# Layer 0 of a two-layer graph network: maxima over two blocks instead of four, sums three blocks late, destination breaks made in pieces

## The chip, the cores and the metric

The kernel runs on one core of a Trainium2 chip. The core has five engines with their own instruction streams: PE (TensorE: matrix products and transposes), DVE (VectorE), ACT (ScalarE), POOL (GpSimd, which here issues the indirect gathers) and SP (SyncE, which here issues the plain transfers). Each engine takes its instructions in the order of the program and stops at the first that has to wait. The metric is the device time of one execution in microseconds.

## The reference

6250 nodes of 128 features, and 106250 edges sorted by destination (50000 drawn pairs in both directions, and a loop at each node). Two layers, each with a layer norm, a relu and a residual sum around it. Cut to what matters:

```python
# layer 0, attention over the edges of each destination
xl = x @ Wl + bl;  xr = x @ Wr + br;  e = edge_attr @ We
m = leaky_relu(xl[src] + xr[dst] + e, 0.2)
logits = m @ att
mx = segment_max(logits, dst)
ex = exp(logits - mx[dst])
den = segment_sum(ex, dst)
out = segment_sum(xl[src] * (ex / (den[dst] + 1e-16))[:, None], dst) + bias_out
h = gelu(x + out); batch norm over the nodes
# layer 1, messages
em = relu(layer_norm(concat(x[src], x[dst]) @ msg_w + msg_b)) * edge_weight
messages = segment_sum(em, dst) / (count + 1e-8)
h_new = relu(layer_norm(concat(x, messages) @ upd_w + upd_b));  gated mix with x
```

## The kernel before

The edges are padded to 128 x 832 and cut into 104 blocks of 1024 edges (8 tiles of 128; `NS` = 104, `ST` = 8). As the edges are sorted, the destinations of a block lie in a window of 126 nodes. The changed part is the loop over the rounds of layer 0. Round `s` works on block `s` for the logits and on block `u = s - LAG` for the sums:

- SP loads the window of `xr` (`W`), the destinations spread over all partitions (`dlb`) and a row of weights for block `s+2` (`load`, L851 to L859). DVE makes the transposed one-hot `oht` of it (`one_hot_t`, L863).
- POOL gathers eight tiles of `xl[src]` into `gl` (L196), from a pool of 10 buffers.
- PE multiplies `oht` with `W` into PSUM, eight products a block (`expand`, L867, called by `spread` for block `s+1`).
- DVE adds the gathered rows (L1033), ACT takes the Relu (L1034), DVE multiplies with att (L1051) and sums over the features (L1053): the logits. Each of these blocks of instructions stands where it is written in the loop, since the scheduling is manual.
- `maxima` turns the logits of `SB` = 4 blocks into exponents and run maxima: it transposes them (L900, PE), scans forward and backward over the runs of equal destinations (L907, L908, DVE), joins the runs across rows (L911 to L926), scans once more with what comes from the rows beside it (L929 to L933), takes Exp (L934, ACT), transposes back (L937, L938) and writes `exm` (L942 DVE, L944 ACT). It is a generator of eight pieces; a round takes two of them, one after the Relu and one at its end.
- The sums of block `u`: DVE makes the one-hot `oh` (L1040) and copies the pair of columns (L1043), ACT scales the gathered rows by the exponents, eight instructions (L1049), and PE multiplies (L1063). One round later `flush` copies the sum from PSUM (L1008, ACT) and SP stores it into one of two result tables.
- `nodes` joins the two tables for a group of four tiles of nodes once their blocks are stored, one step a round over seven rounds; `turn` transposes tiles of `x`.

`LAG` is SB + 3 = 7. `kbrk` holds the breaks between runs of equal destinations, one row per tile of a group of blocks, for the scans. Before the loop it is filled in four pieces of up to seven groups (L832, L833), then scaled (L835). The result tables are zeroed by 20 transfers per layer from SP (L848), in layer 0 four a round over the first five rounds. After the loop come a middle part (batch norm and the tables of layer 1) and layer 1, whose rounds have the same plan without maxima. They are not changed.

Of the kernel before, what the change touches and what calls it, by code (L numbers as in the profile page):

```python
# [30 lines left out]
ST = 8  # L31
SE = ST * P
NS = K // ST
SB = 4
NBT = SB * ST
BT = K // NBT
WIN = 126
# [11 lines left out]
def kernel(  # L49
# [36 lines left out]
    def flat(v, ap, offset=0):  # L86
        return bass.AP(tensor=v.tensor, offset=v.offset + offset, ap=ap)
# [86 lines left out]
    def over_tiles(row, n):  # L174
        return row[:, None, :].to_broadcast([P, n, D])
# [565 lines left out]
    def fast():  # L741
# [39 lines left out]
        att8 = fs.tile([P, D], F32, name="att8")  # L781
        V.tensor_scalar(att8, att_r, 0.8, None, op0=ALU.mult)
        g0 = ExitStack()
        gp = g0.enter_context(tc.tile_pool(name="e0g", bufs=10))
        with tc.tile_pool(name="col1", bufs=1) as p1, tc.tile_pool(name="rows", bufs=2) as rp, tc.tile_pool(
            name="ps_p", bufs=2, space=PSUM
        ) as ps_p:
            base_f = p1.tile([NS, 1], F32, name="base_f")
            V.tensor_copy(base_f, dst_r[:, 0:1])
            fr = rp.tile([NS, SE], F32, name="fr", tag="rows")  # L790
            V.tensor_scalar(fr, dst_r, base_f, None, op0=ALU.subtract)
            dl_b = p1.tile([NS, SE], BF16, name="dl_b")
            V.tensor_copy(dl_b, fr)
            nc.sync.dma_start(dl_d, dl_b)

            for w in Ws:
                nc.scalar.dma_start(w[WIN : WIN + 1], We)
                nc.scalar.dma_start(w[WIN + 1 : P], flat(br, [[0, 1], [1, D]]))
            for o in ohts:
                V.memset(o, 1.0)  # L800
            ends_i = p1.tile([1, 2, K], I32, name="ends_i")
            nc.scalar.dma_start(ends_i[:, 0, :], flat(dst, [[1, 1], [P, K]]))
            nc.scalar.dma_start(ends_i[:, 1, :], flat(dst, [[1, 1], [P, K]], P - 1))
            ea_r = rp.tile([NS, SE], F32, name="ea_r", tag="rows")
# [12 lines left out]
            fst = rp.tile([NS, SE], F32, name="fst", tag="rows")  # L817
            V.memset(fst[:, 0:1], 1.0)
            V.tensor_tensor(fst[:, 1:SE], dst_r[:, 1:SE], dst_r[:, 0 : SE - 1], ALU.not_equal)
            columns(ps_p, fst_c, fst, "ctp")  # L820
            ew_r = rp.tile([NS, SE], F32, name="ew_r", tag="rows")
            nc.sync.dma_start(ew_r, flat(edge_weight, [[SE, NS], [1, SE]]))
            columns(ps_p, ew_c, ew_r, "ctp")


            V.memset(kbrk[:, :, 0:1], 0.0)
            V.memset(kbrk[:, :, P : P + 1], 0.0)
            HB = 7
            for b in range(0, BT, HB):
                n = min(HB, BT - b)  # L830
                dst_n = p1.tile([NBT, HB, P], I32, name="dst_n")
                nc.sync.dma_start(dst_n[:, :n, :], flat(dst, [[P, NBT], [P * NBT, n], [1, P]], b * P * NBT))  # L832
                V.tensor_tensor(kbrk[:, b : b + n, 1:P], dst_n[:, :n, 1:P], dst_n[:, :n, 0 : P - 1],  # L833
                                ALU.not_equal)
            V.tensor_scalar(kbrk[:, :, 1:P], kbrk[:, :, 1:P], -BIG, None, op0=ALU.mult)  # L835
            V.memset(jn, 1.0)
            V.memset(kS, 1.0)
            V.memset(kR, 1.0)
            V.tensor_tensor(jn[:, 1:K], ends_i[:, 0, 1:K], ends_i[:, 1, 0 : K - 1], ALU.not_equal)
            V.tensor_tensor(kS[:, 1:K], ends_i[:, 1, 1:K], ends_i[:, 1, 0 : K - 1], ALU.not_equal)  # L840
            V.tensor_tensor(kR[:, 0 : K - 1], ends_i[:, 0, 1:K], ends_i[:, 0, 0 : K - 1], ALU.not_equal)
            for t in (jn, kS, kR):
                V.tensor_scalar(t, t, -BIG, None, op0=ALU.mult)

        def zero(tables, n, i):

            for r in tables:
                nc.sync.dma_start(r.rearrange("(p k) f -> p (k f)", p=P)[:, i * 5 * n : (i + 1) * 5 * n],  # L848
                                  zt[:, : 5 * n])
# [36 lines left out]
        with tc.tile_pool(name="e0", bufs=2) as ep, tc.tile_pool(  # L886
# [3 lines left out]
        ) as ps_m, tc.tile_pool(name="ps_1", bufs=1, space=PSUM) as ps_1, tc.manual_schedule():  # L890
            iota_ps = ps_1.tile([P, P], F32, name="iota_ps")
            S.copy(iota_ps, iota_f)
            LAG = SB + 3
            gls, lgc, exm, wins, pss, aggs = {}, {}, {}, {}, {}, {}

            def maxima(b):
# [46 lines left out]
                                fst_c[:, bs, :], ALU.mult)  # L943
                S.copy(em[:, :, :, 1], tz[:, 1, :].rearrange("p (s j) -> p s j", j=ST))  # L944
                exm[b] = em
                yield
                yield

            def nodes(g):
# [58 lines left out]
                S.copy(agg, aggs.pop(s))  # L1008
                store(agg, res0_d, s)

            steps, group = None, None
            due = rounds_of(LAG)
            turns = {r + 6: g for r, g in due.items() if g < NGR - 2}
            turns.update({3: NGR - 2, 8: NGR - 1, 13: NGR})
# [5 lines left out]
            for s in range(NS + LAG + 1):  # L1020
                u = s - LAG
                if s + 2 < NS:
                    wins[s + 2] = load(op_, xr_d, s + 2, True)
                if s < NS:
                    gl = gp.tile([P, ST, WL], F32, name="gl")
                    gls[s] = gl
                    for j in range(ST):
                        gather(gl[:, j, :], xl_d, src_c[:, s, j : j + 1])
                if s + 1 < NS:
                    spread(s + 1)  # L1030
                if s < NS:
                    ps = pss.pop(s)
                    V.tensor_tensor(ps, ps, gl[:, :, :D], ALU.add)  # L1033
                    S.activation(ps, ps, AF.Relu)  # L1034
                if steps is not None:
                    next(steps, None)
                if 0 <= u < NS:
                    b, q = divmod(u, SB)
                    oh = ep.tile([P, ST, P], F32, name="oh")
                    V.tensor_tensor(oh, over_tiles(iota_ps, ST), over_features(dl_c[:, u, :], ST),  # L1040
                                    ALU.is_equal)
                    glw = ep.tile([P, ST, W0], F32, name="glw")
                    V.tensor_copy(glw[:, :, D:], exm[b][:, q])  # L1043
                if u >= 1:
                    flush(u - 1)
                if 0 <= u < NS:
                    glu = gls.pop(u)
                    for j in range(ST):
                        S.activation(glw[:, j, :D], glu[:, j, :D], AF.Copy, scale=exm[b][:, q, j, 1:2])  # L1049
                if s < NS:  # L1050
                    V.tensor_tensor(ps, ps, over_tiles(att8, ST), ALU.mult)  # L1051
                    lr = small.tile([P, ST], F32, name="lr")
                    V.tensor_reduce(lr, ps, AX.X, ALU.add)  # L1053
                    V.tensor_add(lr, lr, gl[:, :, D])
                    if s % SB == 0:
                        lgc[s // SB] = mp.tile([P, SB, ST], F32, name="lgc")
                    V.tensor_add(lgc[s // SB][:, s % SB, :], lr, eac_c[:, s, :])
                if s + 2 < NS:
                    one_hot_t(*wins[s + 2])
                if 0 <= u < NS:  # L1060
                    aggs[u] = ps_1.tile([P, W0], F32, name="agg_ps")
                    for j in range(ST):
                        T.matmul(aggs[u], oh[:, j, :], glw[:, j, :], start=(j == 0), stop=(j == ST - 1))  # L1063
                if s < NS and s % SB == SB - 1:
                    steps = maxima(s // SB)
                    next(steps, None)
                elif steps is not None:
                    next(steps, None)
                if s < 5:
                    zero(res0_d, W0, 2 * s)  # L1070
                    zero(res0_d, W0, 2 * s + 1)
                if 20 <= s < 30:
                    zero(res1_d, WL, s - 20)
                if s == 30:
                    nc.sync.dma_start(b_d[NP:], zt[:, :D])
                if s in due:
                    group = nodes(due[s])
                if group is not None:
                    next(group, None)
                if s in turns:  # L1080
                    turn(turns[s])
# [303 lines left out]
```

## Time and profile before

| what | value |
|---|---|
| median of 11 runs | 2414.46 us (2405.15 to 2417.61) |
| profiled execution | 2408.61 us, span 2406.8 us |
| busy, share of the span | PE 57%, DVE 68%, ACT 53%, POOL 70% |
| mean granted TensorE clock | 0.766 |
| first gather of layer 0 | 71.3 us |
| first add of layer 0 | 99.7 us |
| last gather of layer 0 issued | 1139.4 us |
| last sums of layer 0 copied from PSUM | 1183.2 us |
| chain that ended last, by engine | POOL 44%, issue 18%, DVE 15%, DMA 13%, PE 6%, ACT 3% |

In the lines of the profile, L12 is line 12 of the kernel; `out<-in` are the names of the tiles; `xN` counts instructions; a bracket gives the idle time of the engine just before an instruction and what ended it. A line of the waits reads: who waited, for whom, microseconds in total, times, the longest. PE's granted clock is 1.00 at full and 0.50 at half speed.

### The profile page before, as it was taken

To read this page: it belongs to the slowest core of one execution; us is meant where nothing else is said; L and a number is where in the kernel's file an instruction comes from. 1 tells how busy PE (TensorE), PEld (TensorE's weight loads), DVE (VectorE), ACT (ScalarE), POOL (GpSimd) and SP (SyncE) were. 2 spreads that over 40 slices of the span, in tenths; PEclk is the share of its full clock that TensorE was granted. 3 is DMA by queue.
4 is the path that set the end of the run, shared out by engine and by line. 5 is a ranking of instruction groups with operands and counts; after the bars stand their busy time and mean duration, and the time that the engine had idled before them with its cause. 6 is when DMAs were issued, how large, how long until landed. Compare 5 with 4: busy or idle time off the path is not lost.

```text
span 2406.8 us, 30614 instructions
## 1 busy us (share of the span) xinstructions
PE 1372.7 (57%) x7692; PEld 1268.6 (53%) x7692; DVE 1635.9 (68%) x3597; ACT 1277.4 (53%) x4267; POOL 1695.0 (70%) x1703
## 2 busy tenths in 40 slices
PE   6445556556566556665584555555655655555553
PEld 3345555555555555555464555554554655555553
DVE  6666677677677767767545567767767767768765
ACT  5223343333344344334456667677677677667663
POOL 1677777777777777777057777777777777777770
PEclk9668877787878777777686777778778778877876
DMA  6844455444444444443142333343343343334331
GB/s 166 209 117 93 112 150 140 97 99 92 102 101 92 101 95 93 100 99 80 30 140 76 88 96 98 86 106 96 84 108 97 83 109 100 87 102 102 85 97 30
DMA packets 217495, 242.88 MB, mean 101 GB/s; under 512 B 41373, under 2 KB 158077, under 8 KB 217309
## 3 DMA queue, kind: packets, MB, share of 16 engines
q0 software_dynamic: 53792, 110.57, 22.1%
q1 hardware_dynamic: 160657, 130.00, 18.9%
q8 instruction: 63, 1.03, 0.2%
q14 instruction: 123, 1.01, 0.1%
q10 hardware_dynamic: 2860, 0.27, 0.1%
HBM read 197.43 MB, written 43.25 MB: 100 GB/s over the span
## 4 chain that ended last, share of the span: by engine, by line
POOL 44%; issue 18%; DVE 15%; DMA 13%; PE 6%; ACT 3%; POOLq 0%; DVEq 0%; another core or an unknown queue 0%; ACTq 0%; SPq 0%
POOL gl L196 44%; DMA gl<-xl_d,src_c 6%; DMA gl<-a_d,src_c 5%; DVE y L1314 3%; DVE m_ps L1033 2%; DVE y L1298 2%; DVE oh L1309 2%; PE agg_ps L1063 1%; DVE y L1316 1%; PE agg_ps L1329 1%; PE mm L1156 1%; ACT sq L1303 1%; DVE oht L863 1%; DMA src_r<-in_src_dram 1%; PE ctr L1126 1%
## 5 line engine op out<-in xcount | busy, mean ns | idle before, releaser
L196 POOL DMA_INDIRECT gl<-xl_d,src_c x832 | 815.7, 980 | 307.7 <-issue 234.7
L196 POOL DMA_INDIRECT gl<-a_d,src_c x832 | 845.7, 1016 | 260.6 <-issue 236.2
L1329 PE MATMUL agg_ps<-glw,oh 128*128 128x129 f32 x1664 | 362.4, 402 | 493.4 <-ACT glw L1320 454.0
L1329 PEld LDWEIGHTS agg_ps<-glw,oh 128*128 128x128 f32 x1664 | 334.8, 296 | 513.5 <-ACT glw L1320 513.5
L1063 PE MATMUL agg_ps<-glw,oh 128*128 128x130 f32 x1664 | 346.3, 390 | 379.3 <-ACT glw L1049 192.4
L1063 PEld LDWEIGHTS agg_ps<-glw,oh 128*128 128x128 f32 x1664 | 322.4, 291 | 396.4 <-ACT glw L1049 396.4
L1034 ACT ACTIVATE m_ps<-m_ps 128x1024 f32<-128x1024 f32 x104 | 104.8, 1008 | 567.1 <-DVE m_ps L1033 420.4
L1303 ACT ACTIVATE sq<-y 128x128 f32<-128x128 f32 x832 | 257.1, 309 | 274.7 <-DVE y L1298 251.1
L1033 DVE TENSOR_TENSOR m_ps<-m_ps,gl 128x1024 f32<-128x1024 f32 x104 | 128.2, 1232 | 295.3 <-DMA gl<-xl_d,src_c 273.9
L867 PE MATMUL m_ps<-W,oht 128*128 128x128 f32 x1664 | 262.4, 323 | 37.8 <-DVE oht L863 26.4
L867 PEld LDWEIGHTS m_ps<-W,oht 128*128 128x128 f32 x1664 | 246.9, 235 | 46.0 <-DVE oht L863 22.3
L1298 DVE TENSOR_TENSOR y<-y_ps,gl 128x1024 f32<-128x1024 f32 x104 | 126.9, 1220 | 190.5 <-DMA gl<-a_d,src_c 157.6
L1320 ACT ACTIVATE glw<-y,ew_c 128x128 f32<-128x128 f32 x832 | 254.5, 389 | 3.4
L1049 ACT ACTIVATE glw<-gl,exm 128x128 f32<-128x128 f32 x832 | 254.3, 394 | 0.0
L867 PE MATMUL y_ps<-W,oht 128*128 128x128 f32 x1664 | 227.3, 295 | 13.2 <-DVE oht L863 8.9
L867 PEld LDWEIGHTS y_ps<-W,oht 128*128 128x128 f32 x1664 | 223.6, 216 | 13.7 <-issue 13.7
L1314 DVE SCALAR_TENSOR_TENSOR y<-y,rs,mg_r 128x128 f32<-128x128 f32 x832 | 227.5, 345 | 0.0
L863 DVE TENSOR_SCALAR oht<-dlb,iota_p 126x1024 f32<-126x1024 bf16 x208 | 160.2, 770 | 12.7 <-DMA dlb<-dl_d 12.4
L1303 ACT ACTIVATION_READ_ACCUMULATOR sq<-y 128x1 f32 x832 | 155.0, 186 | 0.0
L1051 DVE TENSOR_TENSOR m_ps<-m_ps,att 128x1024 f32<-128x1024 f32 x104 | 129.8, 1248 | 4.8 <-ACT m_ps L1034 4.6
L1317 ACT ACTIVATE y<-y 128x1024 f32<-128x1024 f32 x104 | 109.9, 1057 | 43.0 <-DVE y L1316 42.8
L1316 DVE TENSOR_TENSOR y<-y,mb_r 128x1024 f32<-128x1024 f32 x104 | 127.9, 1230 | 3.6
(251 smaller groups left out, 1606.3 us busy)
## 6 DMA issues: line engine op xcount, KB each, us to landing
dlb<-dl_d SPq DMA_DIRECT2D x208, 256.0 KB
gl<-xl_d,src_c POOLq DMA_INDIRECT x832
gl<-a_d,src_c POOLq DMA_INDIRECT x832
res<-agg SPq DMA_DIRECT2D x104, 64.0 KB
res<-agg SPq DMA_DIRECT2D x104, 63.5 KB
W<-xr_d SPq DMA_DIRECT2D x104, 63.0 KB
W<-b_d SPq DMA_DIRECT2D x104, 63.0 KB
res<-zt SPq DMA_DIRECT2D x20, 325.0 KB
```

Of the source, the lines that this page charges most:

```text
L196: GP.indirect_dma_start(out=dest, out_offset=None, in_=table, in_offset=bass.IndirectOffsetOnAxis(ap=idx, axis=0))
L863: V.tensor_scalar(oht[:WIN, :], dlb[:WIN, :], iota_p[:WIN, :], None, op0=ALU.is_equal)
L867: T.matmul(ps[:, j, :], oht[:, j * P : (j + 1) * P], w, start=True, stop=True)
L1033: V.tensor_tensor(ps, ps, gl[:, :, :D], ALU.add)
L1049: S.activation(glw[:, j, :D], glu[:, j, :D], AF.Copy, scale=exm[b][:, q, j, 1:2])
L1063: T.matmul(aggs[u], oh[:, j, :], glw[:, j, :], start=(j == 0), stop=(j == ST - 1))
L1298: V.tensor_tensor(y, pss.pop(s), gl, ALU.add)
L1303: S.activation(sq, y[:, j, :], AF.Square, accum_out=rs[:, j : j + 1])
L1314: V.scalar_tensor_tensor(yu[:, j, :], yu[:, j, :], ru[:, j : j + 1], mg_r, op0=ALU.mult, op1=ALU.mult)
L1316: V.tensor_tensor(yu, yu, over_tiles(mb_r, ST), ALU.add)
L1320: S.activation(glw[:, j, :D], yu[:, j, :], AF.Copy, scale=ew_c[:, u, j : j + 1])
L1329: T.matmul(aggs[u], oh[:, j, :], glw[:, j, :], start=(j == 0), stop=(j == ST - 1))
```

## The change

`SB` becomes 2: the maxima are taken over 16 tiles (two blocks) at a time, so they run 52 times instead of 26, and a round takes four pieces instead of two: two at its head, one behind the one-hot, one at its end. `LAG` becomes SB + 1 = 3. The empty last piece of `maxima` goes. The pool of `gl` has 8 buffers instead of 10. Within a round the order changes: pieces of the maxima, the one-hot, the copy of the last sums, the columns, the scalings and the sums of block `u` now stand ahead of the add, and the Relu and the product with att follow the add directly. The breaks are made in thirteen pieces of four groups, one before the loop and one at the end of every second round until round 22. The 20 zeroing transfers are issued in the first two rounds.

```diff
-SB = 4
+SB = 2
-        gp = g0.enter_context(tc.tile_pool(name="e0g", bufs=10))
+        gp = g0.enter_context(tc.tile_pool(name="e0g", bufs=8))
+        HB = 4
+        def breaks(pool, i):
+            b = i * HB
+            dst_n = pool.tile([NBT, HB, P], I32, name="dst_n")
+            nc.sync.dma_start(dst_n, flat(dst, [[P, NBT], [P * NBT, HB], [1, P]], b * P * NBT))
+            V.tensor_tensor(kbrk[:, b : b + HB, 1:P], dst_n[:, :, 1:P], dst_n[:, :, 0 : P - 1], ALU.not_equal)
+            V.tensor_scalar(kbrk[:, b : b + HB, 1:P], kbrk[:, b : b + HB, 1:P], -BIG, None, op0=ALU.mult)
...
-            HB = 7
-            for b in range(0, BT, HB):
-                n = min(HB, BT - b)
-                dst_n = p1.tile([NBT, HB, P], I32, name="dst_n")
-                nc.sync.dma_start(...)
-                V.tensor_tensor(kbrk[:, b : b + n, 1:P], dst_n[:, :n, 1:P], dst_n[:, :n, 0 : P - 1],
-                                ALU.not_equal)
-            V.tensor_scalar(kbrk[:, :, 1:P], kbrk[:, :, 1:P], -BIG, None, op0=ALU.mult)
+            breaks(p1, 0)
...
-            LAG = SB + 3
+            LAG = SB + 1
...
-                if s < NS:
-                    ps = pss.pop(s)
-                    V.tensor_tensor(ps, ps, gl[:, :, :D], ALU.add)
-                    S.activation(ps, ps, AF.Relu)
-                if steps is not None:
-                    next(steps, None)
+                step()
+                step()
                 if 0 <= u < NS:
                     b, q = divmod(u, SB)
                     oh = ep.tile([P, ST, P], F32, name="oh")
                     V.tensor_tensor(oh, over_tiles(iota_ps, ST), over_features(dl_c[:, u, :], ST),
                                     ALU.is_equal)
-                    glw = ep.tile([P, ST, W0], F32, name="glw")
-                    V.tensor_copy(glw[:, :, D:], exm[b][:, q])
+                step()
                 if u >= 1:
                     flush(u - 1)
                 if 0 <= u < NS:
+                    glw = ep.tile([P, ST, W0], F32, name="glw")
+                    V.tensor_copy(glw[:, :, D:], exm[b][:, q])
                     glu = gls.pop(u)
                     for j in range(ST):
                         S.activation(glw[:, j, :D], glu[:, j, :D], AF.Copy, scale=exm[b][:, q, j, 1:2])
+                    aggs[u] = ps_1.tile([P, W0], F32, name="agg_ps")
+                    for j in range(ST):
+                        T.matmul(aggs[u], oh[:, j, :], glw[:, j, :], start=(j == 0), stop=(j == ST - 1))
                 if s < NS:
+                    ps = pss.pop(s)
+                    V.tensor_tensor(ps, ps, gl[:, :, :D], ALU.add)
+                    S.activation(ps, ps, AF.Relu)
                     V.tensor_tensor(ps, ps, over_tiles(att8, ST), ALU.mult)
...
-                if 0 <= u < NS:
-                    aggs[u] = ps_1.tile([P, W0], F32, name="agg_ps")
-                    for j in range(ST):
-                        T.matmul(aggs[u], oh[:, j, :], glw[:, j, :], start=(j == 0), stop=(j == ST - 1))
                 if s < NS and s % SB == SB - 1:
                     steps = maxima(s // SB)
-                    next(steps, None)
-                elif steps is not None:
-                    next(steps, None)
-                if s < 5:
-                    zero(res0_d, W0, 2 * s)
-                    zero(res0_d, W0, 2 * s + 1)
+                step()
+                if s % 2 == 0 and (s // 2 + 1) * HB < BT:
+                    breaks(ep, s // 2 + 1)
+                if s < 2:
+                    for i in range(5):
+                        zero(res0_d, W0, 5 * s + i)
```

More of the change, by code (lines that the diff above doesn't have):

```diff
@@ L827, in fast @@
             V.memset(kbrk[:, :, P : P + 1], 0.0)
-            HB = 7
-            for b in range(0, BT, HB):
-                n = min(HB, BT - b)
-                dst_n = p1.tile([NBT, HB, P], I32, name="dst_n")
-                nc.sync.dma_start(dst_n[:, :n, :], flat(dst, [[P, NBT], [P * NBT, n], [1, P]], b * P * NBT))
-                V.tensor_tensor(kbrk[:, b : b + n, 1:P], dst_n[:, :n, 1:P], dst_n[:, :n, 0 : P - 1],
-                                ALU.not_equal)
-            V.tensor_scalar(kbrk[:, :, 1:P], kbrk[:, :, 1:P], -BIG, None, op0=ALU.mult)
+            breaks(p1, 0)
             V.memset(jn, 1.0)
@@ L945, in maxima @@
                 exm[b] = em
-                yield
                 yield
@@ L1009, in flush, with step @@
                 store(agg, res0_d, s)
-            steps, group = None, None
+            steps, group = iter(()), None
+            def step():
+                next(steps, None)
             due = rounds_of(LAG)
```

## The prediction

> **What bounds layer 0 now.** I read the groups of instructions and the chain first: gathers on POOL are the costliest group and the largest share of the chain. Then I asked, for the steady rounds of layer 0 (180 to 1139 us), what POOL waits for, and what DVE waits for.
>
> ```profile
> POOL gl L196 <- issue: 209.7, 688, 0.3
> ```
> ```profile
> L196 POOL DMA_INDIRECT gl<-xl_d,src_c x748 | 731.2, 978 | 228.0 <-issue 209.7 <-DVE rv L931 4.6 <-DMA gl<-xl_d,src_c 3.7
> ```
> ```profile
> DVE m_ps L1033 <- DMA gl<-xl_d,src_c: 247.3, 79, 4.9
> ```
> No gather ever waits over 0.3 us: POOL runs at its own pace, (731.2 + 228.0) / 748 = 1.282 us a gather, 10.26 us a round of eight. DVE is behind it: in the 91.5 rounds from 200 to 1139 us it waits 247.3 us for gathers, 2.70 a round. So a DVE round may grow by 2.7 us for nothing, and every microsecond above that is paid by all the rounds. That is what has to be counted; the timeline gives the pieces.
>
> ```profile
> 111.25 1.23 DVE L1033 TENSOR_TENSOR m_ps<-m_ps,gl 128x1024 f32<-128x1024 f32 x1
> 113.55 1.23 DVE L1051 TENSOR_TENSOR m_ps<-m_ps,att 128x1024 f32<-128x1024 f32 x1 [1.07 <-ACT m_ps L1034]
> ```
> ```profile
> 1008.06 1.23 DVE L1033 TENSOR_TENSOR m_ps<-m_ps,gl 128x1024 f32<-128x1024 f32 x1 [3.07 <-DMA gl<-xl_d,src_c]
> 1009.20 0.14 DVE L929 COPY cc<-tx 32x2 f32<-32x2 f32 x1
> ...
> 1010.78 1.21 DVE L1040 TENSOR_TENSOR oh<-iota_ps,dl_c 128x1024 f32<-128x1024 f32 x1
> 1011.91 0.15 DVE L1043 COPY glw<-exm 128x16 f32<-128x16 f32 x1
> 1011.98 1.21 DVE L1051 TENSOR_TENSOR m_ps<-m_ps,att 128x1024 f32<-128x1024 f32 x1
> ```
> The first fence is a round before any sums: add, then nothing for 1.07 us while ACT does the Relu, then the product with att. The second is a steady round: between add and product stand a step of the maxima and the one-hot, so the Relu costs DVE nothing. Last, PE's instructions (start, then duration) and its work in stretches of 3.41 us, where the second number is PE's busy time and the third from the end is the granted clock:
>
> ```profile
> 637.64 3.79 PE L867 MATMUL m_ps<-W,oht 128*128 128x128 f32 x16 [0.40 <-DVE oht L863]
> 648.05 0.31 PE L937 MATMUL tx<-ident,rv 32*128 32x32 f32 x1
> 656.46 2.05 PE L867 MATMUL m_ps<-W,oht 128*128 128x128 f32 x16 [0.34 <-DVE oht L863]
> 663.72 3.81 PE L1063 MATMUL agg_ps<-glw,oh 128*128 128x130 f32 x16 [5.21 <-DVE glw L1043]
> ```
> ```profile
> 608.01:611.43 3.42, 1.96 (x16) 1.76 (x16) 0.62 (x1) 0.00 (x0) 2.52 (x3) 1.00 0.47 131
> 611.43:614.84 3.41, 1.15 (x8) 1.15 (x8) 3.38 (x6) 2.77 (x9) 2.49 (x4) 1.00 0.27 60
> 614.84:618.25 3.41, 3.41 (x17) 3.18 (x17) 1.95 (x4) 0.83 (x3) 2.77 (x3) 0.50 0.72 142
> ```
> The eight products of an expand take 2.05 us at full clock and 3.79 at half. The clock changes at multiples of 3.41 us: a stretch with 1.96 us of PE work kept it full, one with 1.15 was followed by half.
>
> **The change, part by part.**
>
> *Drain.* From the last add to the last sums' copy the trace has 40 us:
> ```profile
> 1143.19 1.23 DVE L1033 TENSOR_TENSOR m_ps<-m_ps,gl 128x1024 f32<-128x1024 f32 x1 [4.32 <-DMA gl<-xl_d,src_c]
> ```
> ```profile
> 1183.24 0.27 ACT L1008 COPY agg<-agg_ps 128x130 f32<-128x130 f32 x1 [0.58 <-PE agg_ps L1063]
> ```
> Afterwards three sums are left and four turns a round: logits 5.2, transposing them 0.5, a step of nodes 3.3, scans and one-hot 2.1, rows 0.5, sums 2.0 to 3.8, second scans 1.6, Exp with its table load 1.6, transposes and exm 1.0, then two sums of 3 to 4 with a copy each. That makes 25 to 29 us; I take 28 (PE mostly at half clock there). Gain 12 us.
>
> *The round's ring.* The maxima's 14 DVE instructions now come every two rounds, and add, Relu and product stand next to each other behind them. I count one pair of rounds as DVE issues it, starting where the one-hot for the expand ends, with gathers always there.
>
> First round: lt and two scans 0.96 (1029.80 to 1030.76 in the timeline), one-hot 1.13. Meanwhile PE expands, 2.05, and only then transposes fw and rv, 0.25: the row scan starts at 2.3. Rows 0.46, glw 0.1, add at 2.9; add to product 2.30 (111.25 to 113.55); product to the end of the transposed one-hot 3.56 (1011.98 to 1015.54). Sum 8.75. With the expand at 3.7 the row scan waits till 3.95: 10.35.
>
> Second round: cc to the difference 1.58, one-hot 1.13; PE expands 2.05 and transposes 0.42 beside it, so exm starts at 2.7. DVE's exm 0.18, ACT's exm 0.19 behind it, agg copy, then the eight scalings 2.44: ACT is free at 5.6, and only now comes the Relu, which stands behind them in ACT's order; product at 6.65, plus 3.56: 10.2. With the expand at 3.7 the transposes end at 4.15 and all moves by 1.4: 11.6.
>
> To the mean of 9.5 (full clock) or 11.0 (half) comes nodes: 0.8 + 3.3 + 0.75 + 0.69 = 5.5 us per group of 8.5 rounds, 0.65 a round. So DVE's round is 10.15 at full and 11.65 at half clock, against 10.26 on POOL. How often is the expand slow? In the trace the sums stand behind PE's idle time and average 313.9 / 1499 x 16 = 3.35 us, 0.74 of the way from 2.03 to 3.81; the expand follows them without a gap and averages 2.44, 0.28 of the way. Afterwards the expand stands behind the idle time, about 3.8 us in either round, so it is nearer the first; I take 0.65. The round becomes 10.15 + 0.65 x 1.5 = 11.1 us. The ends for it are 10.15 and 11.65.
>
> A rule weighed here. The Trainium skill, "TensorE: Matmul & The Clock Gate", Part 1, has the clock fall after a window of about 3.4 us that is idle. By that, a gap of 3.8 would hold a whole idle window only about one time in nine (an estimate from the page's window), the round would be 10.3 and the total some 80 us less than mine. The row above, where 1.15 busy of 3.41 did not keep the clock, speaks against it.
>
> *Front.* Three of four comparisons (1.06, 1.06, 0.81) and the scaling (1.03) leave the prologue, 4 us of DVE, and three dst_n loads leave SP ahead of the dlb loads. Against it the 20 zero DMAs, 325 KB each, sit in two rounds instead of five: SP takes 0.63 us for each (2.50 for four), they move 6.5 MB at the 330 GB/s seen there, 20 us, and the dlb loads of the next rounds and the second dst_n stand behind them on SP. What is queued behind DVE's waits for these is everything. The fourth add stood at 119.6; I put it at 121, between 116 and 131. Twelve pieces of breaks then cost 0.7 (635 columns took 0.81, 508 are less) and 0.2 each in the rounds; ten of them come after that add: 8 us. dst_n's later loads lie beside 10 us of round and are free unless SP is late.
>
> *POOL and buffers.* Eight gl buffers and a lag of three let POOL run four rounds, 41 us, ahead. When DVE is later than that, gathers wait for the scalings on ACT; this costs nothing more, since DVE sets the pace. A gather beside two scans took 1.12 us instead of 0.94; twice as many scans would add at most 0.2 us to every other round, and only if POOL still set the pace.
>
> *Sum.* Fourth add 121, 100 rounds of 11.1, breaks 8, drain 28: last copy at 1267 instead of 1183.2. The middle and layer 1 (1224 us) are untouched and shift. So +84 us. The profiled execution took 2408.61 (span 2406.8), 5.85 below the median of 2414.46; its time would become 2493, and for the median I say **2498**.
>
> **Rivals.**
> 1. *POOL still paces, faster.* PE stays at full clock because its work is spread more evenly, DVE's round is 10.15 and the first lag is made up; last copy 1143.2 + 28 or a little less, -12 to -16 us, 2400. For it: PE's total work is the same. Against: the margin is 0.1 us a round. It decides where the ring falls to 10.26 us (121 + 8 + 28 + 100 x 10.26 = 1183, break-even too).
> 2. *Expand as fast as today.* Share 0.28, round 10.57: last copy 1214, +31, 2445. For it: sums are then short and near; against: the order within PE's cluster turns.
> 3. *Half clock throughout.* 11.65, +139, 2553. For it: half clock is left only after a stretch almost full of work (3.41 above), and the gap between expand and sums now breaks it.
> 4. *The zeros stall DVE longer in front*: the add at 131, +10 on any of these.
>
> **How the numbers follow.** Mine (round of 10.85 to 11.35, 2470 to 2525) 0.45; rival 2 with all from 10.4 to 10.85, 0.22; rival 3, from 11.35 up, 0.14; rival 1, 0.14; a tie near break-even 0.05. A measurement of this kernel tells about 0.2% from no change. Faster 0.14, same 0.05, slower 0.81. The range 2430 to 2560 leaves out rival 1, the tie and little else.
>
> **What would show it.** The product with att waiting for ACT's Relu in every round (about 1.1 and 2.2 us in turn, some 170 us); the add no longer waiting for gathers; row scans and exm waiting for PE's tx transposes; gathers waiting for ACT's glw by some 40 us in all; expands averaging about 3 us. I am wrong if the add still waits for gathers throughout layer 0, or if the expand stays near 2.1.

## The result, and the profile after

The changed kernel takes 2490.7 us (median of 8 runs, 2487.99 to 2495.11), the kernel before beside it 2414.21 us: 1.0326 times as long, 95% interval 1.0310 to 1.0341. The forecast was 2498 us.

The profiled execution took 2498.04 us, its span 2496.2 us. Layer 0 in the two profiled executions:

| | before | predicted | after |
|---|---|---|---|
| first add | 99.71 | | 102.30 |
| fourth add | 119.56 | 121 (116 to 131) | 131.07 |
| mean of the next 100 rounds, breaks included | 10.24 | 11.18 | 11.06 |
| last add | 1143.19 | | 1237.13 |
| last add to last sums' copy | 40.05 | 28 | 28.75 |
| last sums' copy | 1183.24 | 1267 | 1265.88 |

(11.18 is 11.1 and 8 us of breaks over 100 rounds; 11.06 is (1237.13 - 131.07) / 100.) From the last copy to the end it is 1225.4 before and 1232.2 after, work that was not changed; this execution is the longest of the changed kernel's ten (2485.32 to 2498.04 us).

First the chain of the changed kernel by engine, and two waits of POOL from 130 to 1240 us. POOL had 44% of the chain; now PE, ACT and DVE share it, and gathers wait for the scalings that free their buffers: 70.8 us, which before were 0.

```profile
POOL 28%; DVE 28%; issue 12%; PE 12%; DMA 10%; ACT 9%; SPq 1%; DVEq 0%; another core or an unknown queue 0%; POOLq 0%; ACTq 0%
```
```profile
POOL gl L196 <- issue: 205.1, 673, 0.3
POOL gl L196 <- ACT glw L1052: 70.8, 41, 5.4
```

DVE's waits in the same stretch (total, times, longest). Before, its one large wait was the add's for gathers, 247.3 us. That is 3.3 us now, and in its place stand the Relu and PE's transposes of the maxima.

```profile
DVE m_ps L1060 <- ACT m_ps L1059: 144.1, 100, 2.1
DVE srow L919 <- PE tx L915: 69.4, 47, 2.1
DVE exm L945 <- PE tx L941: 36.0, 36, 1.6
...
DVE m_ps L1058 <- DMA gl<-xl_d,src_c: 3.3, 14, 0.5
```

PE's groups from 180 to 1230 us. An expand is 16 of the instructions in the first line: 316.3 / 1520 x 16 = 3.33 us, before 2.44. A sum of a block, the second line, is 3.07 us, before 3.35.

```profile
L870 PE MATMUL m_ps<-W,oht 128*128 128x128 f32 x1520 | 316.3, 394 | 129.7 <-DVE oht L866 69.8 <-DVE cc L932 58.6 <-DMA dst_n<-in_dst_dram 0.6
L1055 PE MATMUL agg_ps<-glw,oh 128*128 128x130 f32 x1514 | 290.6, 367 | 85.9 <-ACT glw L1052 47.5 <-DVE glw L1049 38.4
```

One pair of rounds in the timeline (start, duration, idle time before and what ended it), the lines of its two waits only:

```profile
707.32 2.45 ACT L1052 ACTIVATE glw<-gl,exm 128x128 f32<-128x128 f32 x8
...
709.67 1.01 ACT L1059 ACTIVATE m_ps<-m_ps 128x1024 f32<-128x1024 f32 x1
...
710.71 1.23 DVE L1060 TENSOR_TENSOR m_ps<-m_ps,att 128x1024 f32<-128x1024 f32 x1 [1.80 <-ACT m_ps L1059]
...
714.33 3.78 PE L870 MATMUL m_ps<-W,oht 128*128 128x128 f32 x16 [0.20 <-DVE oht L866]
...
718.06 0.18 PE L915 MATMUL tx<-ident,rv 16*1 16x16 f32 x1
718.29 0.18 DVE L919 TENSOR_TENSOR_SCAN srow<-kS,tx 1x16 f32<-1x16 bf16 x1 [1.91 <-PE tx L915]
...
721.26 1.23 DVE L1060 TENSOR_TENSOR m_ps<-m_ps,att 128x1024 f32<-128x1024 f32 x1 [1.07 <-ACT m_ps L1059]
```

In the one round the Relu stands behind the eight scalings on ACT, and the product waits 1.80 us. In the other the transposes stand behind an expand of 3.78 us on PE, so the row scan waits 1.91 us, and then the product 1.07 us for the Relu, with nothing between to fill it.

The trace holds a test of the clock's share by itself. I fitted the 88 rounds from the thirteenth to the hundredth, each from add to add, by the length of its expand and the number of the `nodes` instructions in it. A round grows by 0.63 or 0.73 us (the two kinds of round) per us of expand: between 2.05 and 3.79 us that is 1.1 to 1.3 us, and with a short expand and no nodes the round is 9.5 or 9.8 us. That is a correlation within one execution, not a proof; the experiments below change the order and the clock.

### The profile page after: what moved, and what is told of

It is laid out like the page before. It is cut to its first block, busy times and chain, and to the rows that moved or that the text cites. A ratio compares the mean times of both kernels' runs of the same rounds, so it can differ in the third digit from the quotient of the medians.

```text
span 2496.2 us, 31517 instructions
## 1 busy us (share of the span) xinstructions
PE 1469.4 (59%) x7874; PEld 1338.4 (54%) x7874; DVE 1728.4 (69%) x3982; ACT 1289.2 (52%) x4319; POOL 1695.5 (68%) x1703
## 3 DMA queue, kind: packets, MB, share of 16 engines
q0 software_dynamic: 53792, 110.57, 20.8%
## 4 chain that ended last, share of the span: by engine, by line
POOL 28%; DVE 28%; issue 12%; PE 12%; DMA 10%; ACT 9%; SPq 1%; DVEq 0%; another core or an unknown queue 0%; POOLq 0%; ACTq 0%
POOL gl L196 28%; PE m_ps L870 7%; DMA gl<-a_d,src_c 4%; DVE m_ps L1060 4%; DVE lr L1062 4%; DMA gl<-xl_d,src_c 4%; ACT glw L1052 4%; ACT m_ps L1059 3%; DVE y L1319 3%; DVE m_ps L1058 2%; DVE oht L866 2%; DVE y L1303 2%; DVE oh L1314 1%; PE agg_ps L1055 1%; DVE y L1321 1%
## 5 line engine op out<-in xcount | busy, mean ns | idle before, releaser
L1334 PEld LDWEIGHTS agg_ps<-glw,oh 128*128 128x128 f32 x1664 | 334.8, 297 | 516.3 <-ACT glw L1325 516.3
L870 PE MATMUL m_ps<-W,oht 128*128 128x128 f32 x1664 | 345.2, 393 | 146.0 <-DVE oht L866 80.2
L870 PEld LDWEIGHTS m_ps<-W,oht 128*128 128x128 f32 x1664 | 320.3, 296 | 162.6 <-DVE oht L866 97.1
L1055 PE MATMUL agg_ps<-glw,oh 128*128 128x130 f32 x1664 | 325.0, 372 | 95.2 <-ACT glw L1052 53.6
L1055 PEld LDWEIGHTS agg_ps<-glw,oh 128*128 128x128 f32 x1664 | 301.9, 271 | 105.6 <-ACT glw L1052 69.8
L870 PE MATMUL y_ps<-W,oht 128*128 128x128 f32 x1664 | 229.6, 298 | 13.3 <-DVE oht L866 8.6
L1058 DVE TENSOR_TENSOR m_ps<-m_ps,gl 128x1024 f32<-128x1024 f32 x104 | 128.2, 1233 | 23.7 <-issue 14.9
L937 ACT ACTIVATE fw<-fw 16x128 f32<-16x128 f32 x52 | 16.1, 309 | 237.2 <-DVE fw L936 217.0
```

The source lines that it names most:

```text
L870: T.matmul(ps[:, j, :], oht[:, j * P : (j + 1) * P], w, start=True, stop=True)
```

## The experiments

On the chips where the experiments ran, the kernel before took 2986 to 3040 us, not 2414. The record numbers these chips 0, 2 and 5 and does not name the one of the runs above, which I call the first chip; chip 0 itself took 2986.02 us in one session and 3039.6 in a later one, so it is not known whether the chip or the time makes the difference. An undisturbed comparison of whole times was not to be had, and the first thing to learn is what differs there.

**The kernel before and the changed kernel on these chips.** No edit.

> The kernel before, unchanged, for its trace on these chips. If the halts belong to the chip and not to any change, it shows them too: some 35 to 45 of them in layer 0, 150 to 250 us in all, with gathers that wait for ACT's scalings after each; and a fourth add later than 130 us. If it shows none, the 2986 us come from somewhere else, such as a slower gather (more than 1.28 us each).

> The changed kernel itself, beside the kernel before on the chips of the experiments, where the kernel before takes 2986 to 2994 us and PE, DVE and ACT stand still together for 4 to 11 us about every 30 us. If these halts only add the same time to both kernels, 80 to 85 us more than before: ratio 1.026 to 1.030. If they grow with the number of steps that hand work from one engine to another (52 maxima instead of 26), as the 1.041 to 1.049 of the kernels with two blocks so far suggests: 1.040 to 1.055. In rounds without a halt I expect the round of the first pair of traces or somewhat more, 10.9 to 12.1 us, and the product with att waiting for the Relu.

Measured: the kernel before 2987.13 us in this one execution; the changed kernel 3126.8 us against 2989.91, ratio 1.0454 (1.0411 to 1.0497). The gathers have not become slower (0.94 us and 0.30 between them, as before), but POOL waits for ACT in both kernels. The first line is of the kernel before, the second of the changed one, 200 to 1500 us:

```profile
POOL gl L196 <- ACT glw L1049: 284.0, 39, 31.7
```
```profile
POOL gl L196 <- ACT glw L1052: 370.7, 45, 9.7
```

What holds them up looks like this in the changed kernel:

```profile
417.49 0.19 PE L929 MATMUL tx<-ident,crow 1*16 1x1 f32 x2
...
417.61 0.66 PE L1000 MATMUL np<-ident,x_sb 128*128 128x128 f32 x4
...
421.43 3.56 PE L870 MATMUL m_ps<-W,oht 128*128 128x128 f32 x16 [3.17 <-issue]
...
422.21 0.68 DVE L990 BATCH_NORM_STATS2 bns<-h_sb 128x6 f32<-128x512 f32 x1
...
429.00 0.15 DVE L932 COPY cc<-tx 16x2 f32<-16x2 f32 x1 [6.12 <-remote]
429.06 0.59 ACT L1001 COPY x_sb<-np 128x512 f32<-128x512 f32 x1 [11.28 <-remote]
```

PE's transposes for DVE's cc ended at 417.68 and those for ACT's copy at 418.27; both copies start at 429.0, though their engines were free, and the trace names no releaser ("remote"). Where nothing is late, 0.05 us lie between (718.24 to 718.29 in the pair of rounds above). The trace also holds the moments at which the semaphore counted up that PE raises for these steps: 428.98 and 429.04 us, and 429.20 us for the expand that ended at 425.00. So PE's signal comes late, or the ends of PE's products, which the profile models, are later than it shows.

I call it a halt when PE's products, DVE and ACT are idle together for over 2 us. In the kernel before I count 62 in layer 0 from 200 us on (295 us in all); on the first chip there are 5 (12 us). With the add first (below) the hand-off is nearly always the same: 45 of the 46 pairs of rounds from 200 to 1500 us have it at cc.

So the expectation for the kernel before was right about the halts and too low in their number (62 instead of some 40) and their sum (295 us instead of 150 to 250). For the changed kernel the ratio "1.040 to 1.055" held, but not the reason given for it, more halts: by the same count the changed kernel has 47, 163 us in all, fewer than the kernel before. Why the cost here is larger than 1.0326 is open.

What can still be compared on these chips is the length of the rounds between halts. In what follows a round runs from one add to the next, from the thirteenth on, and is *free* if no halt falls into it. Shorter delays stay in, and the changed kernel's free rounds are longer here (13.1 us on average, 47 of 91, where I expected 10.9 to 12.1) than on the first chip (11.1). The kernel before has free rounds of 7.5 us here (57 of 91): after a halt gathers lie ready and DVE runs at its own pace, which the prediction put at 10.26 - 2.70 = 7.56 us. The two kinds of round must be kept apart, because with some of the kernels the halts fall mostly into one of them.

**The add first.** The changed kernel with add and Relu back at the head of the round:

```diff
                 if s + 1 < NS:
                     spread(s + 1)
+                if s < NS:
+                    ps = pss.pop(s)
+                    V.tensor_tensor(ps, ps, gl[:, :, :D], ALU.add)
+                    S.activation(ps, ps, AF.Relu)
                 step()
...
                 if s < NS:
-                    ps = pss.pop(s)
-                    V.tensor_tensor(ps, ps, gl[:, :, :D], ALU.add)
-                    S.activation(ps, ps, AF.Relu)
                     V.tensor_tensor(ps, ps, over_tiles(att8, ST), ALU.mult)
```

> The changed kernel with one thing put back: the add and the Relu stand at the head of the round again, ahead of the steps of the maxima; blocks of two, lag of three, front and buffers stay changed. My theory (the ring of DVE, ACT and PE inside a round is what costs, and it only passes POOL's 10.26 us because the Relu stands bare between add and product and, in every second round, behind the eight scalings): DVE's round falls to about 9 us, the add waits for gathers again (over 0.5 us a round), rounds take 10.26, last sums copied near 1174 us, ratio to before 0.996 (0.991 to 1.002). Rival (twice as many maxima are the cost, whatever the order): no gather waits, rounds over 10.7, ratio 1.02 or more.

> The changed kernel with the add and the Relu back at the head of the round, ahead of the pieces of the maxima; two blocks, lag of three, breaks and zeros stay as changed. On a chip where the kernel before takes about 2414 us. My theory (POOL paces at 10.26 us a round, and the changed order puts 1.1 to 2.2 us of Relu on DVE's path): DVE's round falls back to about 9.6 to 10.2 us, POOL paces again, the drain of 28 us stays: ratio to the kernel before 0.991 to 1.002, product with att waiting for the Relu less than 10 us in all, the add waiting for gathers again. Rival (the second set of 26 maxima, with more work and more waits for PE, is what costs): 1.02 or more, with srow and exm still waiting for PE's tx by over 80 us. From the chip where the kernel before took 2986 us and this one 1.043 times as much: if the same holds here, the rival is right.

Measured: 1.0431 (1.0402 to 1.0460) and, on another chip, 1.0412 (1.0385 to 1.0438). Both are the ratio that the rival had named, the second set of maxima as the cost, and my theory's was missed; nor does the add wait for gathers again (0.4 us in all in the second run, whose waits these are). The rival's sign in the waits is not there: srow and exm wait 12.9 us for PE's tx in all, not over 80, and 54.1 us more for "remote". The product does not wait for the Relu any more, as I had expected. DVE's largest wait is the halt at one place:

```profile
DVE cc L932 <- remote: 475.9, 45, 13.3
```

The free rounds last 9.0 us (45 of them), but they are all of one kind, from an even block's add to an odd one's; the other kind holds the halt each time. So that both kinds together would come below POOL's 10.26 us is not shown by this run, and neither theory nor rival is ruled out for the first chip.

**The order alone.** The kernel before, four blocks, lag seven and ten buffers, with the changed order within the round: add and Relu behind the sums and directly ahead of the product. No other edit.

> The kernel before with the new order inside the round alone (sums ahead of the add; add, Relu and product next to each other); maxima over four blocks, lag of seven, ten buffers, front as before. My theory: the bare Relu adds 1.1 to 1.8 us to a DVE round that has 2.7 us to spare, so POOL still paces, the add still waits for gathers by about 1 us a round; ratio 1.000 (0.995 to 1.004). Rival (the bare Relu costs by itself, 1.07 us in 104 rounds): ratio 1.046.

Measured: 1.0025 (1.0006 to 1.0045). With the maxima over four blocks the new order costs next to nothing in whole time on these chips. It is not free for DVE, though: the free rounds last 10.4 us (55 of 91), 2.9 us more than those of the kernel before and more than the 1.1 to 1.8 us that I had expected. That is about the whole 2.70 us that DVE had to spare on the first chip; whether POOL would still pace there is not shown.

**Ten buffers.** The changed kernel with `bufs=10` instead of 8 for `gl`.

> The changed kernel with ten gather buffers instead of eight. My theory: POOL's 71 us of waiting for ACT's scalings is a consequence of DVE's pace, so POOL's waits shrink by about 20 us and the time stays: ratio to before 1.032 (1.029 to 1.036). Rival (POOL is held up by the buffers and still sets the pace): the 71 us come back, ratio 1.003 to 1.01.

Measured: 1.0489 (1.0450 to 1.0529), the changed kernel itself, on another chip, 1.0454 (1.0411 to 1.0497). That is outside both ranges and on the far side from the rival's. More buffers win nothing here, as it has to be if POOL's waits for the scalings follow from the late rounds and don't cause them; POOL's waits did not shrink either (385.3 us, 370.7 with eight buffers).

**Four blocks.** Two constants of the changed kernel; all the rest, its order too, stays (the lag is then five):

```diff
-SB = 2
+SB = 4
...
-        HB = 4
+        HB = 2
```

> The changed kernel with maxima over four blocks again (SB 4, so a lag of five; two groups of breaks a piece, still thirteen pieces); its order within the round, its 8 buffers, its zeros and its breaks stay. My theory (neither the order nor the two blocks alone cost, only both together lengthen DVE's round past POOL's 10.26 us): two of four rounds have no pieces of the maxima and last 7.6 to 8.7 us, the mean round of DVE is below 10.26, POOL paces, the drain is some 5 to 8 us shorter than before: ratio to the kernel before 0.992 to 1.003, with or without the halts. Rival (the order alone, Relu and product behind the maxima, is the cost, whatever the number of blocks): 1.015 to 1.035.

Measured: 1.0128 (1.0096 to 1.0159), between the two ranges. The two rounds of four that have no pieces of the maxima last 8.2 and 7.7 us, as I had expected, and a third kind 12.9 (13 free); the fourth holds a halt every time. So the mean of the free rounds, 9.05 us (59 of 91; the changed kernel's 13.06), leaves the fourth kind out. (0.0454 - 0.0128) / 0.0454, some 70% of what the change costs on these chips, goes away with the number of blocks (and the lag and the size of the pieces of breaks that follow from it) alone. Its product waits 284 us for the Relu, up to 12.6 us at a time, and ACT's copies of the sums, behind which the Relu stands, wait 296.0 us for "remote": they are what is halted now.

**Four blocks, the add first, an earlier front.** As the four-block kernel above, with the add first, the zeros over five rounds as in the kernel before, and `ew_r` loaded early into a buffer of its own.

> The one before with the add and the Relu at the head of the round, the zeros two a round and table over five rounds as in the kernel before, and the row of layer 1's edge weights loaded early into a buffer of its own. My theory: POOL paces, the drain is 5 to 8 us shorter and the fourth add comes no later than in the kernel before: 0.990 to 1.000, the fastest of all kernels here. Rival (lag, buffers or breaks in pieces cost something that the two blocks have hidden so far): above 1.003.

Measured: 1.0055 (1.0027 to 1.0083). That is the rival's range, and the fourth add came at 168.4 us, later than the kernel before's 164.2. It does not beat the kernel before here, and none of the versions did. Lag five and eight buffers may leave less room to be halted in than lag seven and ten; I have not tested it.

**A warm PE.** The changed kernel with eight products of `ident` with itself into a second half that the PSUM tile of `iota` is given for it, behind the sums of each block:

```diff
...
+                    for j in range(8):
+                        T.matmul(warm, ident, ident, start=True, stop=True)
```

> The changed kernel with eight products of two constant tiles added on PE behind each block's sums, written to a spare half of a PSUM bank that nobody reads: PE works on through its idle gap. My theory (65 to 80% of expands run at half clock because PE idles 3.4 us ahead of them, and DVE waits for them): granted clock over 0.9 in layer 0, expands near 2.1 us, DVE's waits for tx transposes gone, rounds 10.2 to 10.4; last sums near 1192, ratio 1.004 (0.997 to 1.012). Rival (the clock does not matter to the ring, DVE's own work does): ratio stays at 1.03 or grows, as PE has more to do.

> The changed kernel with eight dummy matrix products of ident with itself behind the sums of each block, so that PE has more work in each stretch of 3.41 us. Theory that the half clock of the expands sets the length of DVE's round: expands average near 2.2 us instead of 3.33, granted clock above 0.80, round about 10.3 us, ratio to the kernel before 0.997 to 1.012. Rival (the order of DVE, ACT and PE alone, at either clock, makes the round): ratio 1.028 to 1.045, as with the changed kernel or a little more, since the dummy products take PE time (at least 0.8 us a round) ahead of the transposes.

Measured: 1.0650 (1.0603 to 1.0696) and 1.0664 (1.0632 to 1.0697). Against the changed kernel on these chips this is 0.02 slower, so the dummy products win nothing in whole time: my theory's ratio was missed both times, and it grew, as the first rival had said. The clock rose less than I had expected: 0.77 from 200 to 1500 us in both, 0.63 in the changed kernel, not over 0.9 and 0.80. The expands did get shorter, from 297.3 / 1452 x 16 = 3.28 us to 221.8 / 1405 x 16 = 2.53, and the free rounds from even to odd from 14.7 to 13.6 and 13.3 us. Within them it is 11.1 and 10.8 us where the expand took under 2.6 us (12 and 15 rounds), 14.9 and 15.1 where it took over 3.3 (29 and 25). Within these kernels a slow expand goes with a longer round; the total does not follow it.

**The Relu ahead of the scalings.** The changed kernel with add and Relu of block s issued ahead of the scalings and the sums of block u:

```diff
                     glu = gls.pop(u)
+                if s < NS:
+                    ps = pss.pop(s)
+                    V.tensor_tensor(ps, ps, gl[:, :, :D], ALU.add)
+                    S.activation(ps, ps, AF.Relu)
+                if 0 <= u < NS:
                     for j in range(ST):
                         S.activation(glw[:, j, :D], ...)
...
                 if s < NS:
-                    ps = pss.pop(s)
-                    V.tensor_tensor(ps, ps, gl[:, :, :D], ALU.add)
-                    S.activation(ps, ps, AF.Relu)
                     V.tensor_tensor(ps, ps, over_tiles(att8, ST), ALU.mult)
```

> The changed kernel with the add and the Relu of block s issued ahead of the eight scalings and the sums of block u, on DVE and ACT, everything else as changed. My theory: in every second round the Relu no longer stands behind the scalings (2.45 us) on ACT, so the product waits 1.07 us in both rounds instead of 1.07 and 1.80 to 2.1; the round gets 0.3 to 0.5 us shorter on average, which is 30 to 50 us of 104 rounds where nothing halts, and 11.1 to 11.4 us in the shortest quarter of the rounds instead of 11.6. Rival (the scalings and sums come later instead and hold the buffers): no shorter rounds. Beside the halts of these chips I expect a ratio of 1.030 to 1.046 by my theory, where the changed kernel had 1.045.

**The transposed one-hot early.** The changed kernel with `one_hot_t` moved up between the Relu and the product:

```diff
                     S.activation(ps, ps, AF.Relu)
+                    if s + 2 < NS:
+                        one_hot_t(*wins[s + 2])
                     V.tensor_tensor(ps, ps, over_tiles(att8, ST), ALU.mult)
...
-                if s + 2 < NS:
-                    one_hot_t(*wins[s + 2])
```

> The changed kernel with the transposed one-hot of block s+2 made between the Relu and the product instead of behind the logits; everything else as changed. My theory (in the changed order the expand, 3.8 us at half clock, stands between the transposed one-hot and PE's transposes of the maxima, and so on DVE's path; and the Relu leaves DVE idle 1.07 us): the one-hot fills 0.75 us of the wait for the Relu, PE expands beside the product and the reduction, and the row scan, cc and exm no longer wait for PE. Rounds without a halt fall from 13.2 us (mean; 11.6 the shortest quarter) to 9 to 10, as with the add first (9.0; 8.0). Ratio here 1.035 to 1.046, as that kernel's 1.041; without halts it would be 0.99 to 1.00. Rival (the Relu behind the scalings is most of it): 12 to 13 us and waits for PE's tx as before.

Measured: 1.0618 (1.0542 to 1.0693) and 1.0658 (1.0585 to 1.0730), both slower in whole time than I expected. But the free rounds became shorter. With the Relu ahead of the scalings the shortest quarter lasts under 9.7 us (11.1 to 11.4 expected, 11.6 in the changed kernel); with the one-hot early the mean is 10.8 us, short of the 9 to 10 that I had expected. Mean length by kind over the rounds 13 to 100, with the number of rounds; the last two columns go to the last round. The rows are of different chips and sessions: the changed kernel's is of chip 2, ten buffers of chip 0, the last two of chip 0 in the session in which the kernel before took 3039.6 us.

| kernel | odd to even add | even to odd add | free rounds with an expand under 2.7 us | all rounds |
|---|---|---|---|---|
| changed, first chip | 11.3 (44) | 11.0 (44) | 0.11 | 11.09 |
| changed | 12.4 (28) | 14.7 (16) | 0.09 | 14.18 |
| ten buffers | 12.2 (33) | 14.3 (17) | 0.08 | 14.01 |
| Relu ahead of the scalings | 10.1 (28) | 10.8 (18) | 0.76 | 14.88 |
| one-hot early | (1) | 10.9 (37) | 0.54 | 15.05 |

Two waits and PE's group show how, for the Relu ahead of the scalings. First DVE's wait for the Relu and for the transposes of the row scan, then the expands (212.2 / 1376 x 16 = 2.47 us):

```profile
DVE m_ps L1062 <- ACT m_ps L1054: 64.5, 60, 1.1
...
DVE srow L919 <- PE tx L915: 7.8, 10, 2.5
```
```profile
L870 PE MATMUL m_ps<-W,oht 128*128 128x128 f32 x1376 | 212.2, 318 | 0.5 <-DVE oht L866 0.2
```

And the same of the changed kernel on these chips:

```profile
DVE m_ps L1060 <- ACT m_ps L1059: 99.4, 61, 2.1
...
DVE srow L919 <- PE tx L915: 45.7, 20, 3.2
```
```profile
L870 PE MATMUL m_ps<-W,oht 128*128 128x128 f32 x1452 | 297.3, 387 | 101.6 <-DVE oht L866 41.4 <-DVE lr L1063 21.0 <-DVE lgc L1066 21.0
```

The wait for the Relu never exceeds 1.1 us now, where it was up to 2.1: this is the 0.4 us a round that I had expected. The other 2 to 3 us came from elsewhere. The sums are later now and the expand follows them with hardly any idle time of PE (0.5 us ahead of all expands, 101.6 in the changed kernel), so it runs mostly at full clock, 2.47 us on average, as it did in the kernel before, and the row scan hardly waits for PE's tx. PE's idle time now stands ahead of the sums, which stay slow (313.3 / 1376 x 16 = 3.64 us). With the one-hot early it is the expand that moves towards the sums, and the scan's wait for tx is gone, but not those of cc and exm for PE (20.8 and 11.9 us). So, as far as free rounds show, the place of the expand, behind PE's idle time, is the larger part of the longer round and the Relu behind the scalings the smaller. How much of the 2 to 3 us is delays under 2 us, which stay in the free rounds, is not shown; the fit on the first chip gave a slow expand 1.1 to 1.3 us.

That the mean round was 14.9 and 15.1 us nevertheless says that on these chips the whole time does not follow the free rounds: kernels with two blocks take 14.0 to 15.1 us a round, whether their free rounds last 9, 10 or 13 us, and kernels with four blocks 12.9 to 13.3.

## Why the prediction was right

The direction, the pace that passes from POOL to DVE and the length of the round were right; the step on the front was not. That the whole came out within 7 us of 2498 is in part luck: the front was 10.1 us longer than I said, the 100 rounds 11.9 shorter, the drain 0.75 longer. Nor is 7 us a fine agreement: the profiled execution, for which I had said 2493, took 2498.04, and the median, for which I had said 2498, was 2490.7.

- *POOL to DVE as what paces.* Right. The add waits 3.3 us for gathers instead of 247.3, and POOL waits for ACT: 70.8 us instead of my 40. I had scans slow a gather to 1.12 us; most gathers beside two scans in the kernel before took 0.94.
- *The round, 11.1.* Measured 11.06 with the breaks, which I had added as 0.08. Its parts: the round at a short expand without nodes 9.5 or 9.8 (I had a mean of 9.5); the price of a slow expand 1.1 to 1.3 (I had 1.5); its share (3.33 - 2.05) / (3.79 - 2.05) = 0.74 (I had 0.65, "nearer the first" end). The last two nearly cancel. Rival 2's share of today, 0.28, should by the same formula have been 0.22; the expand went the other way.
- *Relu waits of 1.1 and 2.2 us, some 170 in all.* 1.07 and 1.80 in the pair shown, 2.1 at most, 144.1 in all. I had the add itself 0.3 us too early behind exm: the columns' copy first waits 0.24 us for ACT's half of exm.
- *The drain, 28.* 28.75.
- *The front, 121.* This is the term that was mis-sized, at the far end of what I gave it: 131.07. This execution came to layer 0 2.7 us later than the other (its first memory clearing on DVE at 72.04 instead of 69.31 us), and from there to the first add it is 30.26 us, before 30.40: the 4 us that leave DVE's prologue were not won. DVE is done at 94.20 and waits 8.11 us for the first add:

```profile
95.40 1.62 PE L208 MATMUL ctp<-ident,ew_r 104*128 104x104 f32 x8 [6.26 <-DMA ew_r<-in_edge_weight_dram]
...
98.06 5.77 PE L870 MATMUL m_ps<-W,oht 128*128 128x128 f32 x32 [1.04 <-ACT ew_c L210]
...
102.30 1.23 DVE L1058 TENSOR_TENSOR m_ps<-m_ps,gl 128x1024 f32<-128x1024 f32 x1 [8.11 <-issue]
```

  The first expand stands on PE behind the transposes of the row of layer 1's edge weights (`ew_r`), whose transfer SP issued at 89.21 us, behind five loads of the loop, instead of at 84.18, behind one. Another 8.9 us come between the first and the fourth add: the three intervals are 5.8, 5.8 and 8.3 before, 7.0, 10.6 and 11.2 after. My step took the first rounds as they were, with 2.5 us of waiting for gathers in them, and looked for the cost on SP's queue. But with two blocks the maxima start after the second add instead of the fourth, so the third and fourth adds stand already behind pieces of them:

```profile
115.73 0.39 DVE L911 TENSOR_TENSOR_SCAN rv<-kbrk,lt 16x128 f32<-16x128 bf16 x1
...
119.21 0.18 DVE L919 TENSOR_TENSOR_SCAN srow<-kS,tx 1x16 f32<-1x16 bf16 x1 [3.05 <-PE tx L915]
...
119.87 1.23 DVE L1058 TENSOR_TENSOR m_ps<-m_ps,gl 128x1024 f32<-128x1024 f32 x1 [0.20 <-DMA gl<-xl_d,src_c]
...
131.07 1.23 DVE L1058 TENSOR_TENSOR m_ps<-m_ps,gl 128x1024 f32<-128x1024 f32 x1
```

  None of the waits between the adds is for the zeros or for a load queued behind them. Rival 4 named the right time, 131, and the wrong cause. Zeros over five rounds alone were not tried.
- *The clock rule.* By my estimate from the page of the Trainium skill ("TensorE: Matmul & The Clock Gate", Part 1) the total came out some 80 us under mine, about 2418. Measured were 2490.7, with an expand over 2.7 us in 89% of the rounds: the trace's row, 1.15 us of work in 3.41 not keeping the clock, decided rightly. The whole trace of the kernel before bears the row out (last section).
- *Layer 0 to the total.* The last copy is 1.1 us earlier than I said, +82.6 us on the profiled executions; the medians differ by 76.5.

What stays open: whether putting the add first or going back to four blocks would have returned to about 2414 us on the first chip. The rounds above allow it, but it could not be measured there. So the trace shows that DVE's round came to pace the loop and what it waits for; which edit costs how much on that chip is argued from free rounds elsewhere. Nor is it known what delays PE's hand-offs on the other chips.

## What to carry to other kernels

When an in-order loop is taken out of the shadow of its slowest engine, count its ring once over every engine, with each instruction's queue neighbours: an instruction that is moved also changes at which clock PE runs the next one, and in the free rounds here that was worth more than the wait which the move made. Count the first rounds by the new schedule and not by the old trace, since a shorter group starts its extra work earlier, and follow every load that changes its place in a queue. And time a candidate beside the old kernel on the same chip: the order of candidates by free rounds and by whole time differed on the chips with halts.

## What the runs showed of the hardware

- The same program took 2414 us in the first runs and 2986 to 3040 us on the chips of the experiments, with the same durations of its instructions (medians of an add 1.23 us, of a gather 0.94 and 0.95, an expand 2.05 to 3.8 where nothing halts it). The difference is mostly idle time, and the unchanged part behind layer 0 has it too (1507.1 us to the end instead of 1225.4). Where I followed it, it lay in hand-offs from PE that arrive late (11.3 us between 417.68 and 429.00 above).
- In the kernel before on these chips there are also stretches in which PE issues single matrix products 2.1 us apart (starts at 716.87, 718.97, 721.07 and 723.17 us), waiting for nothing that the trace shows.
- In the trace of the kernel before on the first chip PE's granted clock changes only at steps of 3.41 us. Of the steps at full clock, the 173 that half clock followed had products for at most 0.52 of their time, the 196 that full clock followed for at least 0.43. Half clock was left only after steps filled to 0.79 or more (172). So it matters where bursts stand: moving the Relu ahead of the scalings left PE the same products and took the free rounds with an expand under 2.7 us from 0.09 to 0.76 of all.
